# A transformer block and a state scan on sixteen images: softmax sums on VectorE, their reciprocals by TensorE, a finer gate, and delta's bfloat16 remainders in PSUM

## The chip, the cores and the metric

The kernel runs on one core of a Trainium2 chip. The core has a matrix engine (TensorE, PE in the profile), VectorE (DVE), ScalarE (ACT), GpSimd (POOL), and SyncE (SP), which here issues all DMAs. The metric is the device time of one launch in microseconds. Each engine runs its own list of instructions in order; semaphores join the lists.

## What is computed

Per image (16 of them, 256 channels, 32x32 pixels, so 1024 tokens) the reference does this, cut to its core:

```python
tok = gn(x) + pos                                  # layer 0: attention and feed-forward
q, k, v = split(layernorm(tok) @ w_qkv)            # 4 heads of 32
tok = (softmax(q k^T / sqrt(32)) v) @ w_out + b_out + tok
x = x + gelu(layernorm(tok) @ w_ff1 + b_ff1) @ w_ff2 + b_ff2 + tok

xs = gn(x) + rel                                   # layer 1: selective scan
ctx = sigmoid(conv3(xs) + gate_b)
u, z = split(xs @ in_proj); u = silu(conv4(u))
dt, Bm, Cm = split(u @ x_proj)
delta = softplus(dt @ dt_proj + dt_b)
h[t] = exp(delta[t] * A) * h[t-1] + delta[t] * u[t] * Bm[t]    # 512 channels x 64 states
y[t] = sum_n h[t] * Cm[t]
x = x + ((y + u * D) * silu(z)) @ out_proj * ctx
```

## The kernel before

**Units.** The recurrence of one image is 256 units. A unit is one VectorE scan instruction (`scan`, L994) over 128 rows (64 states of two channels) and 1024 steps; with 16 images that makes 4096. For each unit, `load` (L954) brings the broadcast product delta*u as a tile "dub", six units ahead; `inputs` (L975) multiplies it by the broadcast Bm ("bt") on POOL, four ahead; `decay` (L979) makes exp(delta*A) two units ahead, as "a": two matmuls of bfloat16 pieces of delta into PSUM (L986), then an exp in place on ScalarE (L988). "a" has two PSUM buffers, so the matmuls of unit n+2 wait for the scan of unit n. `outputs` (L1011) contracts a block of eight units with Cm on TensorE (L1019), ScalarE copies the sums (L1025), and TensorE turns them (L1031): one step a unit over the following block.

**Side work.** While image b is scanned, the rest is done beside it, one step a unit: the first group norm of image b+1 (`first_norm`), the gate and the output of image b-1 (`gate_and_store`, L876), attention and feed-forward of b+1 (`attention_layer`), and the scan's inputs of b+1 (`scan_inputs`). These are generators. Each `yield` carries a share, and `rate_for` scales the shares over one so that all steps fit into 247 units; shares up to one take one unit. So a longer list or longer shares in one place shorten the units of the others. Image 0 is prepared alone, and the last image's gate runs after the last scan. The lists of PE, ACT, DVE and POOL stand in program order (L1125 to L1135), so each step's instructions lie between two scans. SP's list is arranged by a scheduler.

**The places that the change touches.**
- `group_norm` (L272): means by matmul with a constant (`sum_of`, L275), reduced on VectorE (L282).
- Attention scores: `kd`, the difference of the keys' halves (L448), for the row maxima (L453); the exps of scores (L555) and the matmul with values (L535), whose 64 output rows per head hold 32 rows of output and 32 equal rows of softmax sums. `evacuate` (L521) copies the first to `ao` (L523) and the second to `sums` (L524), both on ScalarE. For the first half of the tokens, the second head's copies are made one step later, behind the next exps of scores.
- The sums' reciprocal: rows to DRAM and back as 128x32 (`few`), a reciprocal (L579), to DRAM and back as broadcast rows (L568 to L584), then `ao * sums` (L591) and the output matmul (L600).
- Delta in three bfloat16 pieces: `ps` holds delta in PSUM, `pc[0]` is its cast (L835), L843 takes the cast away from `ps`, `pc[1]` is the cast of the rest (L844), L847 makes `pc[2]` from what is left. The next of four row blocks begins in the same PSUM banks (`begin`, L800: L802, abs L804, exp L805; `more`: L810, L811; `rest`: L815, L816).
- Gate: `(y + u*D)` on VectorE (L883), times silu(z) on POOL (L887), the out-projection in four pieces of four matmuls (`project`, L905), times the context (L916), turned back (L922) and added (L900). `gate_loads` issues the first four of its loads during the group norm.
- Buffers: "dub" has seven slots; "bt" and "ct" (the broadcast Cm) have one each.

```python
        for p in range(3):
            for e in range(2):
                nc.sync.dma_start(dpv[d, p, e], pc[p][e:P:2])
        if d + 1 < ND:
            items = [begin(d + 1, 0)]
        yield 1.1
```

Of the kernel before, what the change touches and what calls it, by code (L numbers as in the profile page):

```python
# [3 lines left out]

# [15 lines left out]
P = 128  # L20
C = 256
KC = C // P
# [28 lines left out]
def attention_then_scan_kernel(  # L51
# [29 lines left out]
    small = pool("small", 2)  # L81
    dutp = pool("dutp", 7)
    blk = pool("blk", 2)
# [62 lines left out]
    ident = const.tile([P, P], F32, name="ident")  # L146
    make_identity(nc, ident)
    avg = const.tile([P, P], F32, name="avg")
    nc.vector.memset(avg, 1.0 / C)
# [122 lines left out]
    def group_norm(src, dst):  # L272
        def sum_of(part, sums, k):
            for h in range(2):
                nc.tensor.matmul(  # L275
                    sums, share, part[:, hs(h)],
                    start=(k == 0 and h == 0), stop=(k == KC - 1 and h == 1),
                )

        def mean_of(sums):  # L280
            m = small.tile([P, NG], F32, name="gn_s", tag="gn_s")
            nc.vector.tensor_reduce(  # L282
                m, sums.rearrange("p (h g t) -> p g h t", g=NG, t=2), AX.XY, ALU.add
            )
            return m

        s = psum("gn_m_ps")
        sum_of(src[0], s, 0)
        yield 1
        sum_of(src[1], s, 1)  # L290
        yield 1
        m = s[:, :NG]
        nc.scalar.copy(m, mean_of(s))
        yield 1
        qs = []
        for k in range(KC):
# [10 lines left out]
        yield 1  # L307
# [61 lines left out]
    def first_norm(b, besides=()):  # L369
# [8 lines left out]
        gn = [work("gn") for _ in range(KC)]  # L378
        yield from along(group_norm(xs, gn), fetches(tok, pos) + [None] * 3 + list(besides))
        for k in range(KC):  # L380
# [4 lines left out]
    def attention_layer(b):  # L385
# [41 lines left out]
        for i in range(2):  # L427
            for hf in range(2):
# [5 lines left out]
                if i == 1:  # L434
                    nc.scalar.copy(k4[:, hs(hf)], ps)
                else:
# [10 lines left out]
        kd = hwork("kd")  # L447
        nc.vector.tensor_tensor(kd, k4[:, hs(0)], k4[:, hs(1)], ALU.subtract)  # L448
        waiting = []
# [71 lines left out]
        def evacuate(pair, hf, e):  # L521
            h, o = 2 * pair + e, 2 * DH * e
            nc.scalar.copy(ao[ts(h, DH), hs(hf)], av[o : o + DH])  # L523
            nc.scalar.copy(sums[ts(h, DH), hs(hf)], av[o + DH : o + 2 * DH])  # L524

# [40 lines left out]

        den = dram.tile([2, HEADS, L], F32, name="den", tag="den")
        nc.sync.dma_start(den[0], sums[::DH, :])  # L568
        few = small.tile([P, HEADS * L // P], F32, name="few", tag="few")
        rows = [den[i].rearrange("h (p c) -> (h p) c", c=HEADS * L // P) for i in range(2)]  # L570
        yield 1
        nc.sync.dma_start(few, rows[0])
        yield 1
        tok = []
        for go in fetches(tok, kept):
            go()
            yield 0.5
        yield 0.5
        nc.vector.reciprocal(few, few)  # L579
        yield 1  # L580
        nc.sync.dma_start(rows[1], few)
        yield 1
        for h in range(HEADS):
            nc.sync.dma_start(sums[ts(h, DH)], den[1, h : h + 1].partition_broadcast(DH))  # L584
            if h % 2 == 1:
                yield 0.5
        yield 0.5
        yield 0.5
        outs = []
        for hf in range(2):  # L590
            nc.vector.tensor_tensor(ao[:, hs(hf)], ao[:, hs(hf)], sums[:, hs(hf)], ALU.mult)  # L591
            for k in range(KC):
                for i, ps in outs:
                    if i == k:
                        t = tok[k][:, hs(0)]
                        nc.vector.scalar_tensor_tensor(t, ps, col("b_out", k), t, ALU.add, ALU.add)
            outs.clear()
            for k in range(KC):
                ps = psum("o_ps")
                nc.tensor.matmul(ps, wout_s[:, 0, ts(k, P)], ao[:, hs(hf)], start=True, stop=True)  # L600
                outs.append((k, ps))
            yield 1.3
        for k, ps in outs:
            t = tok[k][:, hs(1)]
            nc.vector.scalar_tensor_tensor(t, ps, col("b_out", k), t, ALU.add, ALU.add)
        del outs, ps
        yield 1.2

# [5 lines left out]
        for hf in range(2):  # L614
            nc.vector.tensor_tensor(xs[hf], xs[hf], tok[hf], ALU.add)
            ps = psum("f1_ps")
            for k in range(KC):
# [8 lines left out]
        yield 2  # L626
        outs = []
        for hf in range(3):
            for k, ps in enumerate(outs):
                t = xs[k][:, hs(hf - 1)]  # L630
                nc.vector.scalar_tensor_tensor(t, ps, col("b_ff2", k), t, ALU.add, ALU.add)
            outs = []
            for k in range(KC if hf < 2 else 0):
                ps = psum("f2_ps")
                nc.tensor.matmul(ps, wff2_s[:, 0, ts(k, P)], hdn[:, hs(hf)], start=True, stop=True)
                outs.append(ps)
            yield 1.2
        state[b]["xs"] = xs
        state[b]["xr"] = dram.tile([C, L], F32, name="xr", tag="xr")

    def scan_inputs(b):
# [106 lines left out]
        project(0, 1)  # L748
        yield 1
        for d in range(ND):  # L750
# [70 lines left out]
        for d in range(ND):  # L821
# [19 lines left out]
            yield 1.1  # L841
            for hf, (ps, e, s) in enumerate(items):
                nc.vector.tensor_tensor(ps, ps, pc[0][:, hs(hf)], ALU.subtract)  # L843
                nc.scalar.copy(pc[1][:, hs(hf)], ps)  # L844
            yield 1.1
            for hf, (ps, e, s) in enumerate(items):
                nc.vector.tensor_tensor(pc[2][:, hs(hf)], ps, pc[1][:, hs(hf)], ALU.subtract)  # L847
            items, ps, e, s = [], None, None, None
# [9 lines left out]

    GATE = ([0.6, 0.6, 0.4] * ND)[:-1] + [1.3] * 8 + [1]

    def gate_loads(b):
# [10 lines left out]
        ]  # L872
        st["gate"] = ys, us, zs, gs, xs, wo_s, come[4:]
        return come[:4]

    def gate_and_store(b):  # L876
# [20 lines left out]
        def finish():  # L897
            for o, hf, ps in turned:
# [4 lines left out]
            turned.clear()  # L903

        def project(o, k):  # L905
            ps = psum3("m_ps")
            for d in range(ND):
                nc.tensor.matmul(  # L908
                    ps, wo_s[:, d, ts(k, P)], us[d][:, hs(o)],
                    start=(d == 0), stop=(d == ND - 1),  # L910
                )
            return ps

        def join(o, k, ps):
            v = gated[o, k] = hwork("v")
            nc.vector.scalar_tensor_tensor(v, gs[k][:, hs(o)], 1.0, ps, ALU.add, ALU.mult)  # L916

# [9 lines left out]

        work_on = [("p", 0, 0), ("p", 0, 1), ("p", 1, 0), ("t", 0, 0), ("p", 1, 1), ("t", 0, 1), ("t", 1, 0), ("t", 1, 1)]
        joined = []
        for what, o, i in work_on:  # L930
            for j in joined:
                join(*j)
            joined.clear()
            finish()
            if what == "p":
                joined.append((o, i, project(o, i)))
            else:
                turn_back(o, i)
            if come:
                come.pop(0)()  # L940
            yield 1.3
        finish()
        yield 1
# [10 lines left out]
    def load(n):  # L954
        b, k, q, e, i = units[n]
        st = state[b]
        if (k, q, e, i) == (0, 0, 0, 0):
            bt = hst.tile([P, L], F32, name="bt", tag="bt")
            ct = hst.tile([P, L], F32, name="ct", tag="ct")
            for v, lo in ((bt, 0), (ct, NS)):  # L960
# [50 lines left out]
    def outputs(b, k, q, e):  # L1011
        hbuf = now["h", e]
        y2 = hst.tile([P, 4, 256], F32, name="y2", tag="y2")
        for r in range(4):
            for s in range(4):
# [8 lines left out]
                if s == 3:  # L1024
                    nc.scalar.copy(y2[:, r], yb[:, :256])  # L1025
                if s % 2 == 1:
                    yield
# [45 lines left out]
    for n, (b, k, q, e, i) in enumerate(units):  # L1073
# [35 lines left out]
        if n + 2 < len(units):  # L1109
            decay(n + 2)  # L1110
        if at >= (1 if b + 1 < B else 8):
            due -= 1.0
# [78 lines left out]
```

## Time and profile before

| What | us |
|---|---|
| three runs, median (lowest to highest) | 12565.47 (12563.84 to 12583.97) |
| the profiled execution; its span | 12592.85; 12590.8 |
| first scan; last scan ends | 413.7; 12534.3 |
| from one image's first scan to the next's, images 1 to 14 | 765.0 to 774.4 |
| image 15, whose scans run beside a gate only | 609.8 |
| mean of one scan (L994); of one POOL product (L977) | 2.273; 2.404 |
| L843 and L847 together, VectorE, all images | 162 |
| L524, ScalarE, 128 copies of 0.577 | 73.9 |

The trace is of one execution. A row of a group names line, engine, operation, output and inputs, the count, busy us, mean ns of one, and the idle time of the engine just before, with what ended most of it. A row of the timeline gives start, length, engine, line and, in brackets, the wait before it and its releaser. A matmul of 32-bit values stands as two records. The granted TensorE clock, over the whole span 0.82 of full speed, differs by stage.

### The profile page before, as it was taken

What the parts mean: (1) busy time and instruction counts of PE and PEld (TensorE: products, weight loads), DVE (VectorE), ACT (ScalarE), POOL (GpSimd) and SP (SyncE); (2) the same over time, 40 slices, a digit from 0 to 9 for tenths busy, and PEclk for the clock granted to TensorE, in tenths of its full rate; (3) what the DMA queues carried; (4) which work ended last, traced back from release to release, by engine and by line L of the source; (5) the groups of instructions that cost most, each with busy time, mean ns of one, the idle gap of its engine ahead of it and who ended that gap; (6) DMA issues with size and microseconds to landing.
All of it is one profiled execution on the core that took longest, in us unless ns stands there. A gap on an engine that the chain in (4) does not pass through costs nothing.

```text
span 12590.8 us, 419601 instructions
## 1 busy us (share of the span) xinstructions
PE 9574.8 (76%) x183984; PEld 5140.4 (41%) x183984; DVE 11064.3 (88%) x7355; ACT 7506.0 (60%) x10792; POOL 10050.9 (80%) x4233
## 2 busy tenths in 40 slices
PE   6686877868778687886868778687786877868777
PEld 2343434434344343443434344343443434434344
DVE  2788998989989899898989989899898998989998
ACT  3565665656656565665656656566565655656554
POOL 0587878878788787887878878787887878878798
PEclk8887988879788797987879888797887978879756
DMA  1566666676766766666676666766666666676666
GB/s 53 189 229 238 224 221 234 228 243 215 232 235 226 240 225 228 232 226 234 227 238 219 225 233 225 243 218 226 231 227 236 219 225 236 224 239 225 229 238 225
DMA packets 1070400, 2819.80 MB, mean 224 GB/s; under 512 B 324433, under 2 KB 402513, under 8 KB 1068562
## 3 DMA queue, kind: packets, MB, share of 16 engines
q1 hardware_dynamic: 1068562, 2792.97, 65.3%
q8 instruction: 1437, 23.54, 0.8%
q14 instruction: 401, 3.28, 0.1%
HBM read 2513.82 MB, written 261.62 MB: 220 GB/s over the span
## 4 chain that ended last, share of the span: by engine, by line
DVE 37%; PE 31%; issue 13%; ACT 8%; DMA 7%; POOL 3%; SPq 1%; DVEq 0%; POOLq 0%; ACTq 0%
DVE h L994 28%; PE a L986 5%; PE yb L1019 5%; ACT a L988 4%; DMA dub<-dus 3%; POOL dub L977 3%; PE av L535 2%; DVE over L453 2%; PE st_ps L547 2%; PE m_ps L908 2%; PE z_ps L684 2%; PE s_ps L473 2%; DMA xs<-ud 2%; DVE u L720 1%; PE gn_v_ps L275 1%
## 5 line engine op out<-in xcount | busy, mean ns | idle before, releaser
L977 POOL TENSOR_TENSOR dub<-dub,bt 128x1024 f32<-128x1024 f32 x4096 | 9752.7, 2404 | 2130.0 <-DMA dub<-dus 1928.2
L994 DVE TENSOR_TENSOR_SCAN h<-a,dub 128x1024 f32<-128x1024 f32 x4096 | 9166.7, 2273 | 596.0 <-ACT a L988 314.3
L988 ACT ACTIVATE a<-a,acol 128x1024 f32<-128x1024 f32 x4096 | 4466.1, 1090 | 3125.6 <-PE a L986 3065.8
L986 PE MATMUL a<-pieces,pick 48*128 48x512 bf16 x8192 | 1875.8, 448 | 2444.5 <-DVE h L994 2333.4
L1019 PEld LDWEIGHTS yb<-h,cd 128*32 128x32 f32 x131072 | 2433.3, 126 | 2822.9 <-issue 1601.6
L1019 PE MATMUL yb<-h,cd 128*32 128x64 f32 x131072 | 3189.4, 248 | 341.0 <-ACT y L1025 203.3
L986 PEld LDWEIGHTS <-pick 48*128 48x128 bf16 x8192 | 594.4, 95 | 2852.7 <-issue 2194.0
L1025 ACT COPY y<-yb 128x256 f32<-128x256 f32 x2048 | 766.5, 374 | 699.1 <-PE yb L1019 691.4
L1031 PE MATMUL yb<-turn,y 128*32 128x16 f32 x32768 | 590.7, 214 | 5.3 <-issue 4.4
L555 ACT ACTIVATE pt<-st_ps 128x512 f32<-128x512 f32 x1024 | 554.3, 599 | 63.8 <-PE st_ps L547 62.6
L535 PE MATMUL av<-pt,vv 128*64 128x512 f32 x2048 | 588.9, 655 | 3.8 <-ACT sums L524 1.6
L547 PE MATMUL st_ps<-sp 33*128 33x512 f32 x2048 | 573.6, 626 | 3.3 <-ACT pt L555 3.3
L1031 PEld LDWEIGHTS yb<-turn,y 128*32 128x32 f32 x32768 | 572.4, 159 | 6.0 <-issue 4.5
L1035 ACT COPY yo<-yb 128x128 f32<-128x128 f32 x512 | 136.4, 266 | 488.9 <-PE yb L1031 472.3
L734 PE MATMUL g_ps<-xp,w 128*128 128x512 f32 x732 | 406.9, 668 | 0.0
L473 PE MATMUL s_ps<-kd,qm 64*128 64x512 f32 x1022 | 340.6, 612 | 21.2 <-DVE kd L448 14.6
L453 DVE CUSTOM_DVE_ANT_0 over<-s_ps,over 128x512 f32<-128x512 f32 x512 | 325.9, 671 | 24.7 <-PE s_ps L473 24.4
L720 DVE SCALAR_TENSOR_TENSOR u<-up,cwh,u 128x1024 f32<-128x1024 f32 x192 | 295.8, 1541 | 28.0 <-ACT u L712 27.7
L481 ACT ACTIVATE over<-s_ps 128x512 f32<-128x512 f32 x511 | 275.2, 594 | 41.4 <-PE s_ps L473 41.4
L908 PE MATMUL m_ps<-xs,w 128*128 128x512 f32 x504 | 279.2, 704 | 10.2 <-POOL xs L887 9.4
L706 PE MATMUL u_ps<-xp,w 128*128 128x512 f32 x512 | 280.0, 674 | 1.5 <-ACT u L712 1.4
L661 POOL TENSOR_TENSOR xp<-xp,xs 128x1024 f32<-128x1024 f32 x32 | 75.1, 2349 | 254.1 <-DVE xp L313 246.5
(183 smaller groups left out, 7316.7 us busy)
## 6 DMA issues: line engine op xcount, KB each, us to landing
dub<-dus SPq DMA_DIRECT2D x4096, 512.0 KB
dps<-pc SPq DMA_DIRECT2D x384, 128.0 KB
pieces<-dps SPq DMA_DIRECT2D x1024, 48.0 KB
xs<-in_x_dram SPq DMA_DIRECT2D x64, 512.0 KB
xs<-kept SPq DMA_DIRECT2D x64, 512.0 KB
zs<-z SPq DMA_DIRECT2D x64, 512.0 KB
ud<-u SPq DMA_DIRECT2D x64, 512.0 KB
dus<-du SPq DMA_DIRECT2D x64, 512.0 KB
```

The costliest lines, as they stand in the source:

```text
L453: nc.vector.tensor_tensor_reduce(r, s, r, 1.0, -3.0e38, ALU.add, ALU.max, mx[:, at : at + 1])
L473: nc.tensor.matmul(s, qm[c // NJ][r, c % NJ], keys[r], start=True, stop=True)
L535: nc.tensor.matmul(av[ts(e, 2 * DH)], vv[j // (NJ // 2)][:, j % (NJ // 2), 2 * pair + e, :], pts[e], start=(j == 0), stop=(j == NJ - 1),)
L547: nc.tensor.matmul(s, ka[r, ts(j, P)], qa[r, hs(hf)], start=True, stop=True)
L555: nc.scalar.activation(pt, s, AF.Exp)
L977: nc.gpsimd.tensor_tensor(v, v, blocks[units[n][0]]["bt"], ALU.mult)
L986: nc.tensor.matmul(a[:, hs(hf)], w, pieces[r], start=True, stop=True)
L988: nc.scalar.activation(a, a, AF.Exp, scale=acol[:, at : at + 1])
L994: nc.vector.tensor_tensor_scan(now["h", e][:, i, :], decays.pop(n), loaded.pop(n), 0.0, ALU.mult, ALU.add)
L1019: nc.tensor.matmul(yb[ts(g, 32), ts(s, 64)], cd[:, at // 16, ts(c, 32)], hbuf[:, :, at : at + 8], start=(c == 0), stop=(c == 1),)
L1025: nc.scalar.copy(y2[:, r], yb[:, :256])
L1031: nc.tensor.matmul(some[ts(r, 32), x], y2[:, r, x:256:8], turn[:, x], start=True, stop=True)
```

## The change

In words: bt and ct become slots of the dub ring, which grows from 7 to 9. Two group-norm shares become 2. Six of the gate's loads go out early instead of four; the gate's projections go in halves, each product is taken one or two steps after its last matmul, and one turned piece is added per step. kd reads the second keys half from PSUM. The sums are copied by VectorE. Their reciprocal stays on the chip: eight small matmuls put heads by tokens into 128x32, VectorE inverts, ScalarE widens it to 32 rows a head, eight matmuls turn it back into two PSUM banks. Output and second feed-forward matmuls share a routine of single steps. The sum for the block's second residual moves from VectorE to POOL. In delta, `ps` is reduced by a matmul with minus the identity, and ScalarE casts both later pieces. `outputs` moves a quarter step; the last image's gate starts at unit 12 instead of 8.

```diff
-    dutp = pool("dutp", 7)
+    dutp = pool("dutp", 9)
+    less = const.tile([P, P], BF16, name="less")
+    nc.vector.tensor_scalar(less, ident, -1.0, None, ALU.mult)
 ...
         sum_of(src[1], s, 1)
-        yield 1
+        yield 2
 ...
-        yield from along(group_norm(xs, gn), fetches(tok, pos) + [None] * 3 + list(besides))
+        yield from along(group_norm(xs, gn), fetches(tok, pos) + [None] * (2 if besides else 8) + list(besides))
 ...
-        nc.vector.tensor_tensor(kd, k4[:, hs(0)], k4[:, hs(1)], ALU.subtract)
+        nc.vector.tensor_tensor(kd, k4[:, hs(0)], keys, ALU.subtract)
+        yield 1
 ...
-            nc.scalar.copy(sums[ts(h, DH), hs(hf)], av[o + DH : o + 2 * DH])
+            nc.vector.tensor_copy(sums[ts(h, DH), hs(hf)], av[o + DH : o + 2 * DH])
 ...
-        den = dram.tile([2, HEADS, L], F32, name="den", tag="den")
-        nc.sync.dma_start(den[0], sums[::DH, :])
 ...
+        for j in range(NJ):
+            nc.tensor.matmul(ps[:, j], sums[:, ts(j, P)], ident[:, ::DH], start=True, stop=True)
+        yield 2
+        nc.vector.reciprocal(few, ps)
+        nc.scalar.copy(wide_few, few.unsqueeze(3).to_broadcast([P, NJ, HEADS, DH]))
+        yield 2
+        for hf in range(2):
+            ps = psum3("inv_ps")
+            for j in range(NJ // 2):
+                w = wide_few[:, hf * (NJ // 2) + j]
+                nc.tensor.matmul(ps[:, ts(j, P)], w, ident, start=True, stop=True)
+            inv.append(ps)
+            yield 1
+            nc.vector.tensor_tensor(ao[:, hs(hf)], ao[:, hs(hf)], inv[hf], ALU.mult)
 ...
-            nc.vector.tensor_tensor(xs[hf], xs[hf], tok[hf], ALU.add)
+            nc.gpsimd.tensor_tensor(xs[hf], xs[hf], tok[hf], ALU.add)
 ...
-            for hf, (ps, e, s) in enumerate(items):
-                nc.vector.tensor_tensor(ps, ps, pc[0][:, hs(hf)], ALU.subtract)
-                nc.scalar.copy(pc[1][:, hs(hf)], ps)
-            yield 1.1
-            for hf, (ps, e, s) in enumerate(items):
-                nc.vector.tensor_tensor(pc[2][:, hs(hf)], ps, pc[1][:, hs(hf)], ALU.subtract)
+            for p in range(2):
+                for hf, (ps, e, s) in enumerate(items):
+                    nc.tensor.matmul(
+                        ps, less, pc[p][:, hs(hf)], start=False, stop=True, skip_group_check=True
+                    )
+                for hf, (ps, e, s) in enumerate(items):
+                    nc.scalar.copy(pc[p + 1][:, hs(hf)], ps)
+                if p == 0:
+                    yield 1.1
 ...
-    GATE = ([0.6, 0.6, 0.4] * ND)[:-1] + [1.3] * 8 + [1]
+    GATE = ([0.6, 0.6, 0.4] * ND)[:-1] + [1.3] * 9 + [1] * 6
-        st["gate"] = ys, us, zs, gs, xs, wo_s, come[4:]
-        return come[:4]
+        st["gate"] = ys, us, zs, gs, xs, wo_s, come[6:]
+        return come[:6]
 ...
-        work_on = [("p", 0, 0), ("p", 0, 1), ("p", 1, 0), ("t", 0, 0), ("p", 1, 1), ("t", 0, 1), ("t", 1, 0), ("t", 1, 1)]
+        plan = "p000 p001 p010 p011j00 p100 p101j01 t00 p110j10 p111f t01 j11 t10f t11 f f"
 ...
-            bt = hst.tile([P, L], F32, name="bt", tag="bt")
-            ct = hst.tile([P, L], F32, name="ct", tag="ct")
+            bt = dutp.tile([P, L], F32, name="bt", tag="dub")
+            ct = dutp.tile([P, L], F32, name="ct", tag="dub")
```

More of the change, by code (lines that the diff above doesn't have):

```diff
@@ L3 @@
 from itertools import chain, cycle
+from re import findall
 import concourse.bass as bass
@@ L306, in group_norm @@
         del qs, q
-        yield 1
+        yield 2
         v = s[:, :NG]
@@ L435, in attention_layer @@
                     nc.scalar.copy(k4[:, hs(hf)], ps)
+                    keys = ps
                 else:
@@ L564, in attention_layer @@
             yield 1
-        den = dram.tile([2, HEADS, L], F32, name="den", tag="den")
-        nc.sync.dma_start(den[0], sums[::DH, :])
-        few = small.tile([P, HEADS * L // P], F32, name="few", tag="few")
-        rows = [den[i].rearrange("h (p c) -> (h p) c", c=HEADS * L // P) for i in range(2)]
-        yield 1
[L572 to L607, printed above, removed]
+        tok = []
+        few = small.tile([P, NJ, HEADS], F32, name="few", tag="few")
+        ps = psum("few_ps")[:, : NJ * HEADS].rearrange("p (j h) -> p j h", h=HEADS)
+        for j in range(NJ):
+            nc.tensor.matmul(ps[:, j], sums[:, ts(j, P)], ident[:, ::DH], start=True, stop=True)
+        fetch(tok, kept, 0)
@@ new lines, in attention_layer @@
+        yield 2
+        nc.vector.reciprocal(few, ps)
+        wide_few = work("wide_few").rearrange("p (j h d) -> p j h d", j=NJ, h=HEADS)
+        nc.scalar.copy(wide_few, few.unsqueeze(3).to_broadcast([P, NJ, HEADS, DH]))
+        wide_few = wide_few.rearrange("p j h d -> p j (h d)")
+        fetch(tok, kept, 1)
+        yield 2
+        inv = []
+        for hf in range(2):
[5 more added lines that the diff above has]
+            yield 1
@@ new lines, in times, with output, add_to, outputs_of @@
+        def times(hf):
+            nc.vector.tensor_tensor(ao[:, hs(hf)], ao[:, hs(hf)], inv[hf], ALU.mult)
+        def output(w, x, hf, k):
+            ps = psum3("o_ps")
+            nc.tensor.matmul(ps, w[:, 0, ts(k, P)], x[:, hs(hf)], start=True, stop=True)
+            return ps
+        def add_to(to, ps, bias, hf, k):
+            t = to[k][:, hs(hf)]
+            nc.vector.scalar_tensor_tensor(t, ps, col(bias, k), t, ALU.add, ALU.add)
+        def outputs_of(w, x, to, bias, ahead=None):
+            a, c = output(w, x, 0, 0), output(w, x, 0, 1)
+            if ahead:
+                ahead()
+            yield 1.4
+            add_to(to, a, bias, 0, 0)
+            add_to(to, c, bias, 0, 1)
+            a = output(w, x, 1, 0)
+            yield 1
+            add_to(to, a, bias, 1, 0)
+            c = output(w, x, 1, 1)
+            yield 1
+            add_to(to, c, bias, 1, 1)
+            yield 1
@@ L609, in attention_layer @@
+        times(0)
+        yield 1
+        yield from outputs_of(wout_s, ao, tok, "b_out", partial(times, 1))
+        del inv, ps, wide_few
         xs = []
@@ L614, in attention_layer @@
         for hf in range(2):
-            nc.vector.tensor_tensor(xs[hf], xs[hf], tok[hf], ALU.add)
-            ps = psum("f1_ps")
+            nc.gpsimd.tensor_tensor(xs[hf], xs[hf], tok[hf], ALU.add)
+            ps = psum3("f1_ps")
             for k in range(KC):
@@ L626, in attention_layer @@
         yield 2
[L627 to L637, printed above, removed]
+        del f1, ps
+        yield from outputs_of(wff2_s, hdn, xs, "b_ff2")
         state[b]["xs"] = xs
@@ L748, in scan_inputs @@
         project(0, 1)
-        yield 1
+        yield 2
         for d in range(ND):
@@ L897, in finish @@
         def finish():
-            for o, hf, ps in turned:
+            for o, hf, ps in turned[:1]:
                 t = xs[o][:, hs(hf)]
@@ L902, in finish, with project, join @@
                     nc.sync.dma_start(out[b, ts(o, P), :], xs[o])
[L903 to L907, printed above, removed]
+            del turned[:1]
+        banks = {}
+        def project(o, k, part):
+            if part == 0:
+                banks[o, k] = psum3("m_ps")
+            for d in (2 * part, 2 * part + 1):
                 nc.tensor.matmul(
-                    ps, wo_s[:, d, ts(k, P)], us[d][:, hs(o)],
+                    banks[o, k], wo_s[:, d, ts(k, P)], us[d][:, hs(o)],
                     start=(d == 0), stop=(d == ND - 1),
                 )
-            return ps
-        def join(o, k, ps):
+        def join(o, k):
             v = gated[o, k] = hwork("v")
-            nc.vector.scalar_tensor_tensor(v, gs[k][:, hs(o)], 1.0, ps, ALU.add, ALU.mult)
+            nc.vector.scalar_tensor_tensor(
+                v, gs[k][:, hs(o)], 1.0, banks.pop((o, k)), ALU.add, ALU.mult
+            )
         def turn_back(o, hf):
@@ L926, in turn_back @@
             turned.append((o, hf, ps))
-        work_on = [("p", 0, 0), ("p", 0, 1), ("p", 1, 0), ("t", 0, 0), ("p", 1, 1), ("t", 0, 1), ("t", 1, 0), ("t", 1, 1)]
[L929 to L938, printed above, removed]
+        plan = "p000 p001 p010 p011j00 p100 p101j01 t00 p110j10 p111f t01 j11 t10f t11 f f"
+        for what in plan.split():
+            for go in findall("p...|j..|t..|f", what):
+                args = [int(c) for c in go[1:]]
+                if go[0] == "p":
+                    project(*args)
+                elif go[0] == "j":
+                    join(*args)
+                elif go[0] == "t":
+                    turn_back(*args)
+                else:
+                    finish()
             if come:
                 come.pop(0)()
-            yield 1.3
-        finish()
+            yield 1.3 if "p" in what else 1
         yield 1
@@ L1025, in outputs @@
                     nc.scalar.copy(y2[:, r], yb[:, :256])
-                if s % 2 == 1:
+                if s % 2 == 1 and (r, s) != (3, 1) or (r, s) == (3, 2):
                     yield
@@ L1110, in attention_then_scan_kernel @@
             decay(n + 2)
-        if at >= (1 if b + 1 < B else 8):
+        if at >= (1 if b + 1 < B else 12):
             due -= 1.0
```

## The prediction

> **What bounds the kernel now.** I read the page first: busy time, then the chain.
>
> ```profile
> PE 9574.8 (76%) x183984; PEld 5140.4 (41%) x183984; DVE 11064.3 (88%) x7355; ACT 7506.0 (60%) x10792; POOL 10050.9 (80%) x4233
> ...
> DVE 37%; PE 31%; issue 13%; ACT 8%; DMA 7%; POOL 3%; SPq 1%; DVEq 0%; POOLq 0%; ACTq 0%
> ...
> L994 DVE TENSOR_TENSOR_SCAN h<-a,dub 128x1024 f32<-128x1024 f32 x4096 | 9166.7, 2273 | 596.0 <-ACT a L988 314.3 <-PE yb L1019 120.8 <-POOL dub L977 106.0
> ```
>
> VectorE is busiest, and the 4096 scans are most of that. Yet the last-ending chain gives it only 37%: the rest is other engines making VectorE wait. So the question is where VectorE idles. One inner image (number 3, scans from 2693.2 to 3460.0 us, 766.8 us), cut by its stages, asked as windows. Columns: stretch and length, then busy us (and instructions) of PE, weight load, DVE, ACT, POOL, then granted TensorE clock, DMA share, GB/s.
>
> ```profile
> 2693.00:2834.00 141.00, 97.99 (x1651) 55.87 (x1650) 112.01 (x66) 60.59 (x85) 115.65 (x51) 0.76 0.75 260
> 2834.00:2957.00 123.00, 95.56 (x2034) 54.84 (x2032) 117.05 (x112) 77.11 (x116) 99.90 (x43) 0.97 0.60 200
> 2957.00:3087.00 130.00, 118.89 (x2396) 56.29 (x2395) 113.89 (x52) 103.24 (x158) 118.61 (x51) 0.95 0.68 234
> 3087.00:3163.00 76.00, 58.33 (x1162) 31.86 (x1165) 73.09 (x48) 45.12 (x62) 65.30 (x29) 0.80 0.61 202
> 3163.00:3352.00 189.00, 151.41 (x2790) 77.08 (x2782) 175.87 (x111) 114.87 (x158) 163.84 (x65) 0.89 0.72 241
> 3352.00:3441.00 89.00, 54.26 (x1188) 31.64 (x1187) 85.11 (x68) 58.36 (x89) 56.20 (x25) 0.62 0.69 221
> ```
>
> VectorE idles 29 us in the first stretch (group norm and the previous image's gate), 6 in maxima, 16 in attention (TensorE 91% busy), 3 in outputs and feed-forward, 13 in the scan's inputs, 4 in delta, and about 6 in the last 19 us: with 689 us busy, that makes 767.
>
> The mechanism behind each wait: "a" has two buffers, so the decay matmul of scan n+2 waits for the end of scan n, and each engine runs its own list in order. Whatever stands ahead of a decay on TensorE, or ahead of a scan on VectorE, is paid once two scans of slack are gone.
>
> **The change part by part, us per inner image.**
>
> *bt and ct in the dub ring: -4.4.* SP waits for the last reader of the old bt, with the next image's dub loads queued behind it:
>
> ```profile
> 2672.25 1.06 SPq L362 DMA_DIRECT2D xs<-in_x_dram  x2
> 2684.20 0.52 SPq L962 DMA_DIRECT2D bt<-rows  x1
> ...
> 2693.15 4.59 DVE L994 TENSOR_TENSOR_SCAN h<-a,dub 128x1024 f32<-128x1024 f32 x2 [5.92 <-POOL dub L977]
> ```
>
> With a slot of its own bt needs no such wait. I leave 1.5 of the 5.9, since ct (512 KB) is now loaded here too and the 40 us after the next boundary (3500 to 3540) show a DMA share of 0.92. Ends: 0 and -5.9.
>
> *Gate: -9.6.* The table of waits for 2693 to 2834 gives VectorE 6.1 us for xs<-ud and 10.8 for m_ps and o_t. Two more loads go out before the gate, and each "ud" is fetched a turn earlier: I leave 2 (-4.1). The projections block in one piece:
>
> ```profile
> 2766.02 6.37 PE L908 MATMUL m_ps<-xs,w 128*128 128x512 f32 x8
> ```
>
> In halves, with each join two steps after its last matmul, VectorE no longer stands behind them; but the stretch 2764 to 2802 has TensorE busy 35.8 of 38 us, and that work stays. I halve the wait (-5.5). Ends: 0 and -14.
>
> *Group norms: -1 (0 to -5).* A longer share moves the reduction one unit back, but the 6.1 us of matmul (L275) stand before the next decay anyway: the next scan is late instead.
>
> *VectorE work that goes, outputs stage: -3.5.* L615 (two of 1529 ns) moves to POOL; L591 falls from 1178 to about 680 ns twice and L448 from 1158 to 680 (both then read PSUM, as L843 does at 679): 3.05 + 1.0 + 0.5. VectorE's waits on the den round trip (147.0 us over the run, 117.7 of them in image 0, which has nothing to overlap) are (147.0 - 117.7) / 15 = 1.95 per later image. Against this stand 16 transposing matmuls in two passes, priced like L922 (412 ns a record at mixed clock, 267 in its fast groups): 9 us of TensorE in a stage 77% busy; I let 3 of it show. The Trainium skill (GPSIMD Engine Reference, section 4.1 Engine selection) speaks against L615's move: a two-input elementwise operation is about twice as slow there. The trace has 2349 (L661) against 1529 ns, 1.54 times, on an engine that waits 1928 us for DMA in L977. By the rule, with POOL as a bound, the step would cost 4.7 - 3.05 = +1.7; by the row it gains 3.05. I take the row.
>
> *Remainders by TensorE: 0 (-8 to +8).* Gone: L843 and L847, 16 x 0.675 = 10.8 us of VectorE. The Trainium skill (Perfetto Trace Analysis, Identifying the Most-Contended Engine) says to relieve the engine with the highest occupancy; by that the sum is 10.8 x 16 = 173 us off. The delta stretch says otherwise:
>
> ```profile
> 3378.05 1.07 ACT L844 CAST pc<-d_ps 128x512 bf16<-128x512 f32 x2
> ...
> 3379.64 1.25 DVE L847 TENSOR_TENSOR pc<-d_ps,pc 128x512 bf16<-128x512 f32 x2
> ...
> 3380.35 2.07 PE L802 MATMUL d_ps<-dt,wdt 128*128 128x512 f32 x2
> ...
> 3386.24 0.70 DVE L815 SCALAR_TENSOR_TENSOR d_ps<-sp_s,d_ps 128x512 f32<-128x512 f32 x1 [0.34 <-ACT d_ps L811]
> ```
>
> From L843 (3376.26) to the next d's L815 are 10.0 us, and 5.9 of it is a latency: L802 (3380.35), abs, exp, an exp of a, add, relu, then L815. Afterwards: from the scan's end, decay 0.6, first remainders 0.9 (two bf16 matmuls, priced at L986's cold 0.3 to 0.45), pc casts to 2.9, outputs and decay on TensorE to 3.2, second remainders 0.9, behind an exp of a the third cast to 4.9; only then L802, since it takes that bank. With today's 5.9 us from L802 on that is 10.8 to 11.3, while VectorE has only three scans. Three such turns cost about +1 each, and the last d, with no successor, gains 2.7. The relief becomes idle time.
>
> *Sums by VectorE: +25.4 (+12 to +28).* The copy at L524 moves from ScalarE to VectorE; in the built order it sits between two scans and waits for ScalarE's copy of the same PSUM bank, L523. The timeline at such a place now (start us, length us, engine, line):
>
> ```profile
> 3008.28 4.47 DVE L994 TENSOR_TENSOR_SCAN h<-a,dub 128x1024 f32<-128x1024 f32 x2 [0.64 <-PE yb L1019]
> ...
> 3012.10 1.08 PE L535 MATMUL av<-pt,vv 128*64 128x512 f32 x4
> ...
> 3012.21 1.09 ACT L988 ACTIVATE a<-a,acol 128x1024 f32<-128x1024 f32 x1
> 3013.25 0.57 ACT L523 COPY ao<-av 32x512 f32<-32x512 f32 x1
> ```
>
> Today the scan before this place ends at 3010.5 and the next follows at once; the copy could not start before 3013.9. Without TensorE's delay of that moment the list after a scan's end is: decay 0.4, exp to 1.7, L523 to 2.3, copy 0.6 (L524 took 577 ns; VectorE's 128x512 operations from PSUM about 670): next scan at 2.9. Where the first half's second head follows (one place per pair), two exps of scores stand ahead of L523: 4.0. Per pair 2.9 + 4.0 + 2.9 + 2.9 = 12.7, twice 25.4, of which 4.8 is busy. Behind the copy wait the scan, hence the decay two later, hence ScalarE. Idle VectorE time of the stage (16 us) lies in other places, where three or four steps of attention come in a row, so it hides little.
>
> *Shares: +2 (-2 to +5).* The listed shares sum to 285.5 after 272.3, so attention has 47 units where it had 51. There a unit beside TensorE's bound costs only its 1.2 us of matmuls; elsewhere 2.28. Some fill the gate's idle time.
>
> *Longer shares before taps: -1.5* (L720 and L674 wait 3.0 in 3163 to 3441).
>
> Sum: -4.4 - 9.6 - 1 - 3.5 + 0 + 25.4 + 2 - 1.5 = **+7.4**; fourteen inner images: +104. Image 0 has no gate beside it: +25.4 - 3.5 - 1.5, about +20. Image 15 has no attention: bt -4.4, fewer late loads -5, tail -2: -11. Together **+113** on the profiled execution (12592.85, span 12590.8), so 12706 there. That execution was 27 us above the median of the runs, 12565.47; from the median it is 12678, rounded **12680**, 0.9% slower.
>
> **Rivals.**
> *A. The relief comes through* (faster): delta's casts fit into the two scans of slack, and the 10.8 us are gained. For it: ScalarE is only 66% busy in that stretch. Against: the chain above. With the sums as priced it gives 12680 - 15 x 10.8 = 12518. It decides where the next L815 follows the end of that scan within 7.5 us, today's 10.0 less the 2.5 that VectorE is spared.
> *B. Attention hides the copies* (faster): VectorE idles 16 us there; if most of the wait lies in it, the copies cost about 8 an image: 12680 - 15 x 17.4 = 12420. Against: place by place, as above.
> *C. Both chains are longer* (slower still): a colder TensorE (clock 0.62 in delta already) makes each of three turns 2 us longer and each of eight copies 0.5: 6 + 4 an image, 12680 + 150 = 12830.
> *D. The change does not do what it says*: a matmul that did not add to what VectorE left in the bank would change the numbers, not the time.
>
> **Chances.** Forecast 0.55, A 0.17, B 0.13, C 0.15. From no change, 0.2% (25 us) can be told. The forecast's own range, 12580 to 12790, is nearly all slower; with C that gives slower 0.69. Same 0.08, from its low end and A's high one; faster 0.23. The 8-in-10 range takes in A, the upper half of B and the centre of C: 12440 to 12840.
>
> **What would show it.** In attention, eight VectorE waits an image ending on ScalarE ao, of 1.5 to 3.5 us. In delta, VectorE busy about 11 us less and the stretch no shorter. At boundaries, no wait of 6 us for dub. In the gate, hardly a wait for m_ps. I am wrong if attention's stretch is not longer per scan, or if delta's shrinks by 8 us or more.

## The result and the profile after

The changed kernel takes 12902.55 us (median of 4 runs, 12893.71 to 12921.03) against 12571.45 us for the kernel before on the same chip: 1.0264 times as long, 95% interval 1.0247 to 1.0282. The forecast had the direction and not the size: +331 us where +113 was expected, outside its range. In the profiled executions the span goes from 12590.8 to 12895.5 us, +304.7.

The page of the changed kernel, in the order in which the page of before was read: busy time, the chain that ended last, then the costliest groups of VectorE.

```profile
PE 9845.0 (76%) x184720; PEld 5261.2 (41%) x184752; DVE 10954.7 (85%) x7196; ACT 7564.3 (59%) x10808; POOL 10162.3 (79%) x4265
...
PE 38%; DVE 35%; issue 12%; ACT 9%; DMA 4%; POOL 1%; DVEq 0%; SPq 0%; POOLq 0%; ACTq 0%
...
L1009 DVE TENSOR_TENSOR_SCAN h<-a,dub 128x1024 f32<-128x1024 f32 x4096 | 9187.2, 2275 | 867.6 <-ACT a L1003 530.3 <-PE yb L1034 196.2 <-POOL dub L992 79.8
...
L529 DVE COPY sums<-av 32x512 f32<-32x512 f32 x128 | 88.2, 689 | 464.9 <-ACT ao L528 440.3
```

VectorE has 110 us less to do (10954.7 against 11064.3) and the kernel is 305 us longer. Three things stand in these lines. The chain leaves VectorE (37 to 35%) for TensorE (31 to 38%). The scans wait longer for their decay from ScalarE (530.3 us against 314.3). And a new group waits five times its own work: the copies of "sums" on L529, 88.2 us busy and 464.9 us idle ahead of them. Of the idle time 113 us lie in image 0's own attention, where no scan runs yet; beside the scans 120 copies wait 352 us, 2.9 us each.

Where in an image that happens is read from windows. I cut image 3 of the changed kernel at scans 0, 40, 72, 136, 208 and 256 (columns as in the forecast: stretch and length, then busy us of PE, weight load, DVE, ACT, POOL, clock, DMA share, GB/s):

```profile
2768.26:2893.20 124.94, 94.73 (x1712) 54.44 (x1706) 108.90 (x62) 56.46 (x77) 115.80 (x49) 0.76 0.81 287
2893.20:2985.91 92.71, 73.32 (x1457) 40.02 (x1456) 86.70 (x80) 61.66 (x91) 79.00 (x35) 0.93 0.67 213
2985.91:3184.64 198.73, 159.64 (x3113) 79.93 (x3111) 155.78 (x98) 126.00 (x191) 153.16 (x66) 0.87 0.54 183
3184.64:3405.46 220.82, 178.95 (x3120) 93.81 (x3119) 199.45 (x128) 127.36 (x170) 189.17 (x75) 0.85 0.65 223
3405.46:3554.86 149.40, 99.79 (x2117) 55.26 (x2121) 128.71 (x81) 100.15 (x150) 101.92 (x45) 0.72 0.68 230
```

The same cut of the kernel before, first and third stretch:

```profile
2693.15:2836.67 143.52, 100.66 (x1688) 57.07 (x1687) 112.01 (x67) 62.65 (x87) 117.19 (x51) 0.76 0.75 260
...
2926.06:3091.47 165.41, 145.84 (x2990) 74.36 (x2991) 147.61 (x77) 124.64 (x189) 148.14 (x64) 0.93 0.65 225
```

Boundary and gate (scans 0 to 40) went from 143.5 to 124.9 us, as meant. The stretch that holds attention's values (scans 72 to 136) went from 165.4 to 198.7 us while VectorE's work there grew by 8: its idle time rose from 18 to 43 us, and TensorE's granted clock fell from 0.93 to 0.87. Delta (the last stretch) has VectorE 7 us less busy (135.6 before) and is 0.8 us shorter (150.2 before).

### The profile page after: what moved, and what is told of

The parts are those of the page before. It is cut to its first block, busy times and chain, and to the rows that moved or that the text cites. A ratio compares the mean times of both kernels' runs of the same rounds, so it can differ in the third digit from the quotient of the medians.

```text
span 12895.5 us, 420876 instructions
## 1 busy us (share of the span) xinstructions
PE 9845.0 (76%) x184720; PEld 5261.2 (41%) x184752; DVE 10954.7 (85%) x7196; ACT 7564.3 (59%) x10808; POOL 10162.3 (79%) x4265
## 4 chain that ended last, share of the span: by engine, by line
PE 38%; DVE 35%; issue 12%; ACT 9%; DMA 4%; POOL 1%; DVEq 0%; SPq 0%; POOLq 0%; ACTq 0%
DVE h L1009 26%; PE yb L1034 6%; PE a L1001 6%; ACT a L1003 5%; PE st_ps L552 3%; PE av L540 3%; DMA dub<-dus 3%; DVE over L458 2%; PE m_ps L922 2%; PE z_ps L692 2%; PE s_ps L478 2%; PE yb L1046 2%; POOL dub L992 1%; DVE u L728 1%; PE qk_ps L434 1%
## 5 line engine op out<-in xcount | busy, mean ns | idle before, releaser
L1009 DVE TENSOR_TENSOR_SCAN h<-a,dub 128x1024 f32<-128x1024 f32 x4096 | 9187.2, 2275 | 867.6 <-ACT a L1003 530.3
L552 PE MATMUL st_ps<-sp 33*128 33x512 f32 x2048 | 625.7, 691 | 2.8 <-ACT pt L560 2.8
L529 DVE COPY sums<-av 32x512 f32<-32x512 f32 x128 | 88.2, 689 | 464.9 <-ACT ao L528 440.3
L728 DVE SCALAR_TENSOR_TENSOR u<-up,cwh,u 128x1024 f32<-128x1024 f32 x192 | 278.7, 1452 | 33.5 <-ACT u L720 33.2
L692 PE MATMUL z_ps<-xp,w 128*128 128x512 f32 x508 | 277.6, 674 | 1.4 <-ACT z_t L698 1.4
```

What stands on the lines that cost most here:

```text
L552: nc.tensor.matmul(s, ka[r, ts(j, P)], qa[r, hs(hf)], start=True, stop=True)
L1009: nc.vector.tensor_tensor_scan(now["h", e][:, i, :], decays.pop(n), loaded.pop(n), 0.0, ALU.mult, ALU.add)
```

## The experiments

Below, "an inner image" is the mean of images 1 to 14, measured in the trace from scan start to scan start: 768.7 us before, 788.8 after. Ratios compare the medians of several runs with those of the kernel before on the same chip. The two right columns are each from one profiled execution, and such a one can lie off its median: e1's is 33 us below it, e4's 10 and e7's 20 us above.

| run | ratio | 95% interval | inner image | first scan starts |
|---|---|---|---|---|
| before | 1 | | 768.7 | 413.7 |
| after | 1.0264 | 1.0247 to 1.0282 | 788.8 | 427.7 |
| e1 after, sums on ScalarE | 0.9850 | 0.9831 to 0.9869 | 755.0 | 402.9 |
| e2 before, sums on VectorE | 1.0347 | 1.0321 to 1.0373 | 798.4 | 427.2 |
| e3 after, sums copied first | 1.0044 | 1.0029 to 1.0059 | 773.4 | 404.7 |
| e4 after, sums copied a step later | 0.9898 | 0.9881 to 0.9915 | 761.9 | 416.5 |
| e5 e1, remainders on VectorE | 0.9827 | 0.9811 to 0.9843 | 755.9 | 401.8 |
| e6 before, remainders on TensorE | 0.9987 | 0.9978 to 0.9997 | 767.3 | 421.2 |
| e7 e1, gate of before | 0.9905 | 0.9888 to 0.9921 | 762.1 | 416.0 |
| e8 before, bt and ct in the ring | 0.9906 | 0.9890 to 0.9923 | 760.1 | 405.8 |
| e9 before, ring, gate and shares | 0.9807 | 0.9794 to 0.9820 | 753.4 | 427.3 |

### The copies of the sums, undone and alone

e1 is the changed kernel with one line turned back; e2 is the kernel before with the same line turned the other way.

```diff
-            nc.vector.tensor_copy(sums[ts(h, DH), hs(hf)], av[o + DH : o + 2 * DH])
+            nc.scalar.copy(sums[ts(h, DH), hs(hf)], av[o + DH : o + 2 * DH])
```

> The changed kernel with the second copy of a finished bank (the sums) on ScalarE again, everything else kept. Theory 1 (the eight VectorE copies of an image and what follows them, later decays and a colder TensorE, make the stretch of scans 72 to 136 longer by 35 us in each inner image, 31 in image 0, 10 before the first scan): all of that comes back, 14 x 35 + 31 + 10 = 531 us, so 12370 to 12400 us, well below the kernel before. Theory 2 (only the holes between two scans that hold a copy, 29.2 us an image, are the copies' doing): 15 x 29.2 + 10 = 448, so 12455 us. Theory 3 (the holes were sized rightly in the forecast, 25.4 us an image, and the rest of the 35 comes from attention having 47 scans instead of 51): 15 x 25.4 = 381, so 12520 us.

> The kernel before with one edit, the sums copied by VectorE. Theory 1 (the copies and what follows them, whatever the shares): 12571 + 531 = 13100 us. Theory 2 (the holes alone): 12571 + 448 = 13020 us. Theory 3 (part of the cost comes from the denser attention, which this kernel doesn't have): 12571 + 381 = 12950 us or less.

Undone, this one line turns a kernel 2.6% slower than before into one 1.5% faster: 0.985 x 12571 = 12383 us, some 520 below the changed kernel, inside the range of Theory 1 (12370 to 12400). Its rows, busy time and then the two copies of the bank, both on ScalarE:

```profile
PE 9627.3 (78%) x184720; PEld 5176.5 (42%) x184752; DVE 10863.2 (88%) x7068; ACT 7601.6 (61%) x10936; POOL 10160.0 (82%) x4265
...
L529 ACT COPY sums<-av 32x512 f32<-32x512 f32 x128 | 73.9, 577 | 1.7
...
L528 ACT COPY ao<-av 32x512 f32<-32x512 f32 x128 | 73.7, 576 | 7.7 <-PE av L540 5.6
```

On ScalarE the second copy waits for nothing (1.7 us in 128). The window of scans 72 to 136 of image 3 is back to 166.3 us, at a clock of 0.96:

```profile
2872.14:3038.42 166.28, 148.00 (x3015) 74.88 (x3013) 150.62 (x89) 126.06 (x194) 148.40 (x65) 0.96 0.67 215
```

Alone on the kernel before (e2), the copies cost 3.47%, 436 us, with an interval (403 to 469) that holds Theory 2 (448) and not Theory 1 (531) or Theory 3 (381). So their price depends on the rest of the kernel: 29.7 us an inner image there, 33.8 in the changed kernel. (The 10 us before the first scan, in Theories 1 and 2, cannot be put down to the copies: see the end.)

What one such place looks like in the changed kernel, at the first two copies of image 3:

```profile
3056.04 1.10 ACT L1003 ACTIVATE a<-a,acol 128x1024 f32<-128x1024 f32 x1
...
3057.05 0.58 ACT L528 COPY ao<-av 32x512 f32<-32x512 f32 x1
3057.66 0.68 DVE L529 COPY sums<-av 32x512 f32<-32x512 f32 x1 [3.46 <-ACT ao L528]
3058.38 2.29 DVE L1009 TENSOR_TENSOR_SCAN h<-a,dub 128x1024 f32<-128x1024 f32 x1
...
3060.72 0.61 PE L1001 MATMUL a<-pieces,pick 48*128 48x512 bf16 x2 [3.16 <-DVE h L1009]
...
3061.12 1.92 PE L552 MATMUL st_ps<-sp 33*128 33x512 f32 x4
3061.37 1.09 ACT L1003 ACTIVATE a<-a,acol 128x1024 f32<-128x1024 f32 x1 [3.74 <-PE a L1001]
...
3063.14 1.09 ACT L560 ACTIVATE pt<-st_ps 128x512 f32<-128x512 f32 x2 [0.67 <-PE st_ps L552]
3064.24 0.58 ACT L528 COPY ao<-av 32x512 f32<-32x512 f32 x1
...
3064.85 0.69 DVE L529 COPY sums<-av 32x512 f32<-32x512 f32 x1 [4.18 <-ACT ao L528]
```

Read it from below. The copy at 3064.85 waits for ScalarE's copy at 3064.24; ScalarE gets to that after two exps of scores (3063.14), and these wait for the scores (L552), which take 1.92 us here and 1.02 where TensorE runs at the full clock. TensorE itself had just stood 3.16 us, for the scan that the previous copy held up, and its granted clock (third number from the end) was halved after that:

```profile
3050.00:3056.00 6.00, 6.00 (x148) 3.00 (x148) 4.21 (x2) 4.53 (x8) 5.61 (x3) 1.00 0.64 213
3056.00:3061.00 5.00, 1.84 (x38) 0.87 (x40) 2.97 (x2) 1.63 (x3) 4.03 (x3) 0.91 0.61 202
3061.00:3066.00 5.00, 3.05 (x38) 1.22 (x36) 1.12 (x2) 3.13 (x5) 1.70 (x2) 0.50 0.32 108
```

Over images 1 to 14 the hole between two scans at the eight places is 4.20, 4.76, 3.50, 2.95, 2.92, 4.85, 3.13 and 2.93 us, 29.2 together; the same eight places of e1 have 1.0. The other 5.6 of the 33.8 are idle time between other scans: 3.4 in attention and 2.2 behind it.

### The order and the place of the copy

e3 swaps the two lines of the copy, so that VectorE comes first:

```diff
-            nc.scalar.copy(ao[ts(h, DH), hs(hf)], av[o : o + DH])
             nc.vector.tensor_copy(sums[ts(h, DH), hs(hf)], av[o + DH : o + 2 * DH])
+            nc.scalar.copy(ao[ts(h, DH), hs(hf)], av[o : o + DH])
```

e4 puts VectorE's copies off to the next step of attention, where settle() makes those that are owed:

```diff
-            nc.vector.tensor_copy(sums[ts(h, DH), hs(hf)], av[o + DH : o + 2 * DH])
+            owed.append((sums[ts(h, DH), hs(hf)], av[o + DH : o + 2 * DH]))
...
                 for j in range(NJ):
+                    settle()
                     scores = []
```

> The changed kernel with VectorE's copy of the sums put ahead of ScalarE's copy of the outputs from the same bank. If the cost is VectorE's wait for ScalarE's copy (0.58 us each), 128 x 0.6 = 77 us come back: about 12825 us, and the waits of VectorE end on TensorE's av. If it is that the copy stands in VectorE's list ahead of a scan before the bank is finished, little comes back, and ScalarE now waits for VectorE with an exp of a behind it: 12880 to 12950 us.

> The changed kernel with VectorE's copies of the sums put off to the next step of attention, by when the bank has long been finished and copied by ScalarE. If the place in VectorE's list is the whole cost, VectorE hardly waits before a copy (under 0.3 us each), and the 531 us come back less at most the copies' own 128 x 0.69 = 88 us, against ScalarE relieved of 128 x 0.58 = 74 us: 12370 to 12460 us. If work of VectorE in attention costs by itself (the next av then waits for a copy, and TensorE and the decays with it), more than 100 us of it stay: 12500 us or more.

Both times expected of e3 were wrong: the swap gives back 2.2%, 277 us, and not 77 or less. That the waits would end on av came true. The timeline of e3 at the same two places says why:

```profile
2989.84 0.68 DVE L528 COPY sums<-av 32x512 f32<-32x512 f32 x1 [2.86 <-PE av L540]
2990.56 2.29 DVE L1009 TENSOR_TENSOR_SCAN h<-a,dub 128x1024 f32<-128x1024 f32 x1
2990.56 0.57 ACT L529 COPY ao<-av 32x512 f32<-32x512 f32 x1 [0.63 <-DVE sums L528]
2992.88 0.70 DVE L528 COPY sums<-av 32x512 f32<-32x512 f32 x1
```

The second head's copy (2992.88) now waits for nothing, since its bank was finished a step earlier; in the changed kernel it had waited 4.18 us. So the wait was not for the 0.58 us of ScalarE's copy but for ScalarE's whole list ahead of it, the exp of a and the exps of scores. Four of the eight waits of an image vanish, and the four that are left end on TensorE (64 of 128 copies wait on av, 206.7 us, of which 84 lie in image 0 ahead of the first scan).

e4 takes the copy out of the way of the scan, and 0.9898 x 12571 = 12443 us lies inside the lower of its two expectations. Its row of the copies:

```profile
L535 DVE COPY sums<-av 32x512 f32<-32x512 f32 x128 | 88.2, 689 | 131.0 <-ACT ao L528 78.4 <-issue 38.0 <-DMA ys<-yo 6.6
```

Of the 131.0 us of waits 103 lie ahead of the first scan; beside the scans it is 0.23 us a copy. An inner image of the profile is 6.9 us longer than in e1; by the medians (69 us over 15 images) it is 4.6. The copies' own time is 8 x 0.69 = 5.5. So VectorE idles in attention, and still most or all of the extra work there shows in the time.

### Delta's remainders

e5 is e1 with the remainders subtracted by VectorE as before; e6 is the kernel before with the new form alone:

```diff
-            for hf, (ps, e, s) in enumerate(items):
-                nc.vector.tensor_tensor(ps, ps, pc[0][:, hs(hf)], ALU.subtract)
-                nc.scalar.copy(pc[1][:, hs(hf)], ps)
...
+            for p in range(2):
+                for hf, (ps, e, s) in enumerate(items):
+                    nc.tensor.matmul(
+                        ps, less, pc[p][:, hs(hf)], start=False, stop=True, skip_group_check=True
+                    )
...
```

> The changed kernel with the sums copied by ScalarE again and both remainders of delta's pieces subtracted by VectorE again (against the one with only the sums undone, 0.985 of before). Theory of the forecast (the 10.8 us an image that TensorE takes from VectorE turn into idle time of VectorE, and the turns of delta get no longer): no change, 0.983 to 0.987. If the relief is real once attention is not in the way: 16 x 10.8 = 173 us slower, 0.999. If TensorE's remainders lengthen the turns (theory C of the forecast, 6 us an image): 96 us faster, 0.977.

> The kernel before with one edit, both remainders made in the bank by TensorE and cast by ScalarE. Forecast: 0 us an image, 0.998 to 1.002. Relief real: 173 us faster, 0.986. Turns longer by 6 us an image: 1.008.

Both come out near nothing: 0.9827 against 0.9850 with intervals that overlap, and 0.9987 where the relief, if it were real, would have made 0.986. What e6 gains, 16 us (4 to 28 by its interval), is a tenth of the 173; e5 against e1 points the other way. The tables of waits show the exchange in one line (engine, line and what it waited for; us, times, longest), here of the changed kernel and of e6:

```profile
DVE d_ps L823 <- ACT d_ps L819: 189.3, 69, 11.0
```

```profile
DVE d_ps L817 <- ACT d_ps L813: 156.7, 65, 11.0
```

Before, the same wait (its L815 for L811) took 86.1 us in 72 places. So in e6, which differs from before in this edit alone, 71 us of the 161 that L843 and L847 took (80.7 and 80.0 us) are idle time at this one place; in the changed kernel the wait has grown by 103, other edits included. A turn of delta in the changed kernel:

```profile
3452.78 1.03 PE L852 MATMUL d_ps<-pc,less 128*128 128x512 bf16 x2
...
3453.90 1.07 ACT L856 CAST pc<-d_ps 128x512 bf16<-128x512 f32 x2
...
3456.19 0.61 PE L852 MATMUL d_ps<-pc,less 128*128 128x512 bf16 x2
...
3457.32 1.07 ACT L856 CAST pc<-d_ps 128x512 bf16<-128x512 f32 x2
...
3457.96 1.12 PE L810 MATMUL d_ps<-dt,wdt 128*128 128x512 f32 x2 [1.16 <-ACT pc L856]
...
3462.86 0.69 DVE L823 SCALAR_TENSOR_TENSOR d_ps<-sp_s,d_ps 128x512 f32<-128x512 f32 x1 [3.08 <-ACT d_ps L819]
```

10.1 us pass from the first remainder to the next d's L823; before, 10.0 passed from L843 to L815. Over all 48 turns the mean is 10.0 in both kernels (9.65 in e6). The chain runs over TensorE and ScalarE and is about as long as it was.

### Gate and ring

e7 is e1 with the gate of before (plan, shares, four early loads); e8 is the kernel before with the ring alone:

```diff
 # e8
-    dutp = pool("dutp", 7)
+    dutp = pool("dutp", 9)
...
-            bt = hst.tile([P, L], F32, name="bt", tag="bt")
-            ct = hst.tile([P, L], F32, name="ct", tag="ct")
+            bt = dutp.tile([P, L], F32, name="bt", tag="dub")
+            ct = dutp.tile([P, L], F32, name="ct", tag="dub")
```

> The changed kernel with the sums on ScalarE again and the gate of before (its plan, its shares, four early loads and not six). Forecast of the gate: 9.6 us an image, 14 inner images and some 5 in the last: the gain of it goes, 12383 + 140 = 12520 us, 0.996. The cut of the profile by scans gives the stretch of scans 8 to 40 14 us, of which 1 belongs to the group norms: 12383 + 180 = 12565 us, 1.000. If the later stages, which get their places back (attention has 51 scans again and not 47), give it back: 12420 us or less, 0.988.

> The kernel before with one edit, bt and ct in slots of the ring of dub, which has nine buffers. Forecast: 4.4 us an image times 15, 66 us faster, 0.995. By the cut of the changed kernel by scans (2 us in scans 0 to 8): 30 us, 0.998. If the loads just wait elsewhere: 1.000.

The ring is worth nearly twice the 66 us of the forecast, and more than every other reading: 0.94%, 118 us, 8.7 us an inner image of the profile. At the boundary from image 3 to 4 of e8 the queue goes straight on, and the scans with it:

```profile
3403.91 0.52 SPq L962 DMA_DIRECT2D bt<-rows  x1
...
3406.10 0.52 SPq L962 DMA_DIRECT2D ct<-rows  x1
3409.31 3.54 SPq L972 DMA_DIRECT2D dub<-dus  x2
3410.01 18.05 DVE L994 TENSOR_TENSOR_SCAN h<-a,dub 128x1024 f32<-128x1024 f32 x8 [1.63 <-ACT a L988]
```

Before, bt of image 3 was issued 9 us ahead of the image's first scan (2684.20 against 2693.15). Here it goes out 17 us ahead, since image 4 starts at 3421.12, with the sixth scan of this group of eight, and no scan of the group waits. The wait of about 6 us for dub at the boundary is gone whole (some 5.8 us by scan 8), and 1.8 us more come in scans 16 to 24, where VectorE hardly waits any longer for the gate's loads (2.5 us an image before, 0.3 here, in scans 14 to 25), and 1.3 between scans 128 and 144.

The gate is worth less than forecast: 0.55% by e7 against e1, some 70 us, or 5 an inner image; the two profiles give 7.1 (e1's lies below its median and e7's above). By scan 40 the new gate leads by 14.5 us in the profiles. It still leads by 14.3 at scan 168, by 8.4 at scan 200 and by 7.1 at the end. Scans 168 to 200, where 5.9 us are given back, hold most of the taps (the convolution of u, L728). The ratio, 0.9905, is none of the three that were expected: it lies between giving everything back but 40 us (0.988) and the forecast's own gain (0.996).

### What is left of the outputs stage

> The kernel before with bt and ct in the ring, the new gate and the changed shares, and nothing else: the outputs stage (den through DRAM, L615 on VectorE), kd, the remainders and the sums are as before. Against the run with sums and remainders undone (0.9827 of before) it tells what the rebuilt outputs stage is worth by itself. Forecast of that stage: 3.5 us an image, 15 images, some 52 us: this kernel 0.987. Rival: the transposing matmuls and ScalarE's wide copy eat the gain, or it is given back later: 0.981 to 0.983. By the single runs, ring (-8.7 us an inner image) and gate (-7.1) alone give 15.8 x 14 + 20 = 240 us: 0.981.

e9 is the kernel before with ring, gate and the longer shares, and lacks the rebuilt outputs stage, with its kd, that e5 has (remainders and sums as before in both). It is the fastest of all, 0.9807 (0.9794 to 0.9820), and its interval overlaps e5's a little. So the outputs stage gains nothing; that it costs something is not shown. In the inner images e5 leads by 5.0 us between scans 136 and 176, more than was forecast, and loses 7.4 between 176 and 208. VectorE is spared 67.6 us over the run (L615, the products with the sums, kd) and gets 40.3 of them back as longer instructions on SBUF: those that write u take 383.0 us where e9 has 359.6, those that write xs, without L615, 280.0 for 263.1. Between scans 176 and 208, where the 7.4 us are lost, that is the smaller part: VectorE is busy 2.1 us longer there and idles 5.4 us longer (8.0 for 2.6, means of images 1 to 14). Its waits there end on ScalarE (z, u and a). One of them, for the taps' input, in e5 and, under another number, in e9:

```profile
L728 DVE SCALAR_TENSOR_TENSOR u<-up,cwh,u 128x1024 f32<-128x1024 f32 x192 | 276.3, 1439 | 35.9 <-ACT u L720 35.6
```

```profile
L721 DVE SCALAR_TENSOR_TENSOR u<-up,cwh,u 128x1024 f32<-128x1024 f32 x192 | 262.5, 1367 | 5.2 <-ACT u L713 5.0
```

## Why the prediction was wrong

The steps of the forecast beside what the runs gave, in us. The measured values of an inner image are from single profiles, those of the whole run from the ratios, where a step is good to some 20 to 40 us:

| step | inner image, forecast | measured | whole run, forecast | measured | from |
|---|---|---|---|---|---|
| bt and ct in the ring | -4.4 | -8.7 | -66 | -118 | e8 |
| gate | -9.6 | -7.1 | -141 | -69 | e1, e7 |
| norms, shares, taps | -0.5 | +0.5 | -9 | -56 | e9 less ring and gate |
| outputs stage | -3.5 | +2.5 | -52 | +25 | e5, e9 |
| remainders | 0 | -0.9 | 0 | +29 | e1, e5 |
| sums by VectorE | +25.4 | +33.8 | +381 | +520 | after, e1 |
| sum | +7.4 | +20.1 | +113 | +331 | |

The mechanism was right at the step that decides: the place, the wait for ScalarE's copy and the sign. That step was sized too small, and two gains were counted that did not last. In the profiled runs the error lies in the inner images: they grew by 281 us where 104 were put, the start by 14 more, while image 0 (+21) and image 15 with what follows it (-11) came out as forecast (+20 and -11). For image 0 that is luck in part, since the sums alone took 29 there.

**The term that failed: "per pair 2.9 + 4.0 + 2.9 + 2.9 = 12.7".** It was worked out without "TensorE's delay of that moment", that is with a TensorE that starts the decay as the scan ends. The runs showed 15.4 and 13.8 us for the two pairs, and 5.6 us an image in waits elsewhere, for which the forecast had no cost. At the first copy of the first pair TensorE and ScalarE are late with attention itself, so the exp of a ends 2.9 us after the previous scan and not 1.7; where two exps of scores stand ahead, the scores come 0.67 us late from a TensorE that idled and runs at half the clock (1.92 us for 1.02). Rival C had a colder TensorE add 0.5 us a copy; the holes did come out 0.5 a copy longer (29.2 less 25.4, over eight), not all of it by the clock, and with the waits elsewhere it is 1.05 (33.8 less 25.4). Over the profiled run the sums are 14 x 33.8 + 29 (image 0, 767.0 less e1's 737.9) = 502 us where 15 x 25.4 = 381 were put.

**Local gains booked as gains of the whole.** The outputs stage (-3.5) and the gate (-9.6) did what was said within their own stretches (5.0 us in scans 136 to 176, 14.5 by scan 40). The forecast then let them stand to the end of the image. In the taps 7.4 and 5.9 us of this were lost again, for the most part as idle time of VectorE (5.4 us more in e5 than in e9, 6.0 more in e1 than in e7). What makes it wait there when it arrives earlier was not settled. By the ratios this makes errors of 77 us for the outputs stage and 72 for the gate, beside 139 for the sums; the ring (52) and the norms and shares (47) came out better than forecast. For the move of L615 the forecast also took too good a row: where L615 meets no GpSimd instruction (2 of 32 times) it takes 1.22 us and not 1.53, so that GpSimd's 2.35 is nearly twice as long, as the rule that it set aside has it.

**What held.** The remainders were forecast at nothing against the plain sum of 173 us; e5 and e6 leave no room for more than a few tenths of a per cent. The way to the nothing was off: the turns were put at 10.8 to 11.3 us and took 10.0, as before. So the rule of the most contended engine, as it was weighed there, does not carry over to a stretch whose bound is a chain through three engines. Rivals A and B are refuted: hardly any relief came through in delta (e6), and attention hid none of the waits (e1) and little of the copies' own time (e4). Of rival C the half about the copies came, and the half about delta's turns did not. The ring's wait was worth all of its 5.9 us and more; the 1.5 left to the arrival of ct were not needed, and what SP's blocked queue held back further on was overlooked.

The 14 us by which the profiled run starts its scans later can be put down to no edit (see the end).

What stays open: it was not tried to take the order between the two copies of a bank away. The Trainium skill (PSUM — Partial Sum Buffer, PSUM bank collisions raise a hardware error) says that two engines may be in one bank at once where they keep to different quadrants of 32 partitions, and these copies read rows o to o+31 and o+32 to o+63; no run here shows what that would give.

## What to carry to other kernels

Before moving work to an engine that looks idle, ask where in that engine's list it will stand and what it must wait for there: 0.69 us of copying cost 4.2, because it stood between two scans and waited for another engine's list. When a stage is made faster, follow the gain to the end of the period; here some of what was won at one place was lost again at a later one, twice. The cheapest edit, a slot of its own for a load that blocked a queue, was the best of the six.

## What the runs showed of the hardware

The start of the first scan follows the granted clock of TensorE, and no edit sorts it. Between 130 and 260 us, in attention ahead of the first scan, e5 was granted 0.84 and e9 0.62 (third number from the end):

```profile
130.00:260.00 130.00, 113.73 (x352) 36.88 (x352) 12.55 (x23) 56.07 (x98) 4.67 (x2) 0.84 0.07 24
```

```profile
130.00:260.00 130.00, 112.04 (x271) 27.68 (x271) 2.44 (x5) 44.44 (x81) 0.00 (x0) 0.62 0.07 21
```

Their first scans start at 401.8 and 427.3 us, though the two kernels differ there in the outputs stage and kd alone. In all eleven profiles the start follows the clock of this stretch: 402 to 406 us at 0.83 or 0.84, 414 to 421 at 0.72 to 0.74, 427 to 428 at 0.62 to 0.66 (before 0.73, after 0.66). Kernels with the sums on ScalarE stand in all three groups. There is one profile of each kernel, so how far this clock varies among executions of one kernel is not shown. A difference of some 25 us between two single profiles can come from there; the medians of several runs and the length of an inner image are what to compare.

Stalls of one engine lower the clock of another: in scans 72 to 136 of images 1 to 14 the granted TensorE clock was 0.96 in e1, 0.94 in e4, 0.90 in e3 and 0.87 in the changed kernel, in the order of VectorE's waits for the copies. At half the clock four matmuls of scores took 1.92 us for 1.02, which lengthened the next wait.

The same instruction of VectorE on two SBUF operands gets longer where it meets GpSimd's. The gate's L883 (128x1024) takes 1799 ns on average before, 2234 in the changed kernel (its L894) and 2346 in e1, 28 to 35 us over the run. Where it meets no GpSimd instruction it takes 1.28 us (9 of 64 before, 4 in the changed kernel); 25 of 64 overlap with one for more than 1 us before, and 60 in the changed kernel. The Trainium skill (SBUF — State Buffer, Who interferes with whom) says that such an instruction and a GpSimd one that reads SBUF exclude each other on a shared port; the times agree with it, and part of the idle time that an earlier load saves comes back as busy time.
